# Graph attention, layer 2: weighted rows summed by VectorE and TensorE slot by slot, with a GpSimd memset at every sixth gather, in place of 32-node blocks summed on TensorE

## The chip, the cores and the metric

The kernel runs on one core of a Trainium2 chip. The core has five engines with an instruction stream each: TensorE (PE in the profile, its weight loads PEld), VectorE (DVE), ScalarE (ACT), GpSimd (POOL) and SyncE (SP). SP issues the plain DMAs; GpSimd issues the indirect ones, those that fetch or store rows by a list of row numbers. Both kinds are carried out by the same 16 DMA engines. The metric is the time of one execution on the device, in microseconds. Three runs of the kernel before took 5383.51, 5389.56 and 5395.65 us: a median of 5389.56.

## What is computed

Two graph attention layers over 10,000 nodes with 768 features and 170,000 edges (160,000 random ones and a self loop for each node), each with a layer norm and a residual, then a last layer norm:

```python
def gat_conv(x, edge_index, W, a_src, a_dst, bias, heads, out_ch, concat):
    ei = _add_self_loops(edge_index, n)
    src, dst = (ei[0], ei[1])
    xl = (x @ W).reshape(n, heads, out_ch)
    alpha_src = jnp.einsum('nhc,hc->nh', xl, a_src)
    alpha_dst = jnp.einsum('nhc,hc->nh', xl, a_dst)
    e = jax.nn.leaky_relu(alpha_src[src] + alpha_dst[dst], 0.2)
    m = jax.ops.segment_max(e, dst, num_segments=n)
    e = jnp.exp(e - m[dst])
    s = jax.ops.segment_sum(e, dst, num_segments=n)
    alpha = e / (s[dst] + 1e-16)
    msg = xl[src] * alpha[:, :, None]
    out = jax.ops.segment_sum(msg, dst, num_segments=n)
    ...
    return out + bias

h = gat_conv(x, edge_index, W1, a_src1, a_dst1, b1, 4, 256, True)      # layer 1
h = relu(layer_norm(h, g1, be1)) + (x @ Wr1 + br1)
h1 = h
h = gat_conv(h, edge_index, W2, a_src2, a_dst2, b2, 1, 768, False)     # layer 2
h = layer_norm(h, g2, be2) + (h1 @ Wr2 + br2)
x = _layernorm(x + h)
```

All of it is in float32. Layer 2 has one head of 768 columns: for each node, the rows of its sources are weighted with a softmax and summed.

## The kernel before, in words

**Preparation** (up to about 880 us). While TensorE computes x·W1 into table1, VectorE sorts the nodes by their number of edges. The sorted nodes are cut into 79 blocks of 128, one node to a partition. All nodes of a block get the same number of slots, SLOTS[t], from 8 to 41, 1377 in all; a slot that a node does not need points to an empty row. A slot is a row of 128 sources, one for each node of the block. The blocks are taken in the order TURNS: the sizes rise from 8 to 41 in blocks 0 to 39, and fall from 27 to 9 in blocks 40 to 78.

**Layer 1** (880 to about 3445 us) gathers a slot's 128 rows of table1 at a time into a ring of 29 slots, weighs them on ScalarE and VectorE, a part of them on TensorE, and then, in the same stretch, computes the block's rows of table2 (h1·W2, with two columns for the attention). It also stores h1 and x in the new order (h1_d, x_d). `logits` (L488 on) turns the numbers of a block's nodes into the lists of row numbers for layer 2 (L511).

**Layer 2** (`ordered_layer2`, to the end) has a ring of 41 slots of 770 + 1 columns. The first slot of each block holds the block's own rows, which lie together in table2, and comes by a plain DMA on SP's queue (L474). The other 1298 slots are gathers on GpSimd's queue (L445). `Ring.fetch(upto)` issues whatever is not issued yet; each gather waits until the slot it overwrites, 41 earlier, has been read. The order of all instructions is the order in which the program issues them (`manual_schedule`), engine by engine.

Within a block, the n slots are cut into u = n - 4w single ones and w waves of four. A single slot k is as above: partition p holds a source of node p. In a wave, the four slots are rearranged: slot g holds, for the 32 nodes of the quarter g of the block, four sources each. The list of numbers for this is `wide`, made of `slots` by 16 copies (L897). A block then goes like this:

- `exponents(t)` (L960 to L994): the attention logits, their maximum by node, the exponents. The maximum needs moves between quarters of the partitions, for which there are many small VectorE instructions.
- `weighed(t, e)`: VectorE writes `spots` (L1005), a 128x32 matrix for each wave slot that has the weight of each partition's row in its node's column, and adds up the single slots (L1014, L1012). The ring's column 770 is 1, so that the sum of weights comes along.
- `summed(t, spots, acc)`: TensorE multiplies spots with the ring's rows (L1026), four matmuls with 32 output rows for each half and wave, into PSUM.
- `residual(t + 1)` (L1036, L1038): TensorE computes x + h1·Wr2 for the next block, among the sums.
- `norms(t - 1)`, in three steps between these: sum of both parts (L1048), division and bias (L1052), layer norm (L588, L590, L601, L603, L604), the residual (L1056), the last layer norm, whose last step is on ScalarE (L1062), and the scatter into the output by GpSimd (L1063).

`ring.fetch` is called twice a block, after the single slots and after the sums. The first two blocks' x and h1 and a broadcast of br1 lie in the ring's last slots (from slot 35 on) until TensorE has read them.

For the lines after the change: `weigh` (L523), `logits` (L481 on), `normalised`, `norms` and `attend_parts` are shared helpers.

Of the kernel before, what the change touches and what calls it, by code (L numbers as in the profile page):

```python
# [49 lines left out]
QUAD = 32  # L50
# [28 lines left out]
def gnn_kernel(ctx, tc, x, x_cols, src, dst, src_col, dst_col, W1, a_src1, a_dst1, b1, g1, be1, Wr1, br1,  # L79
# [21 lines left out]
    WAVES = [(n - 1) // G for n in SLOTS]  # L101
    SINGLE = sum(n - G * w for n, w in zip(SLOTS, WAVES))
    COLUMN, ALONE, WAVE = [0] * TOTAL, [0] * NT, [0] * NT
    a = w = 0
    for t in TURNS:
        ALONE[t], WAVE[t], u = a, w, SLOTS[t] - G * WAVES[t]
        a, w = a + u, w + WAVES[t]
        COLUMN[FIRST[t]:FIRST[t] + SLOTS[t]] = (list(range(ALONE[t], a))
                                               + list(range(SINGLE + G * WAVE[t], SINGLE + G * w)))
# [87 lines left out]

    def runs(lo, hi):

        q = lo  # L200
        while q < hi:
            e = q + 1
            while e < hi and COLUMN[e] == COLUMN[e - 1] + 1:
                e += 1
            yield COLUMN[q], COLUMN[q] + e - q, q
            q = e

    def prepare():

        with tc.tile_pool(name="prep", bufs=1, side="right") as pool, \  # L210
# [172 lines left out]
            def listed(t, window):  # L383
# [16 lines left out]
                for i in range(m):  # L400
                    f = FIRST[t + i]
                    for c, d, q in runs(f + 1, f + SLOTS[t + i]):
                        nc.vector.tensor_scalar_add(slots[:, c:d], got[:, i, q - f - 1:q - f - 1 + d - c],
                                                    float(NP))
                    c = COLUMN[f]
                    nc.vector.tensor_copy(slots[:, c:c + 1], order[:, t + i:t + i + 1])
# [54 lines left out]
    class Ring:  # L461
# [4 lines left out]
        def __init__(self, pool, table, row, size, own, index, more=0):  # L466
            self.table, self.size, self.own, self.issued, self.index = table, size, own, 0, index
            self.row = row
            self.rows = pool.tile([P, size, row + more], F32, name="ring")

        def fetch(self, upto):
            for q in range(self.issued, min(upto, TOTAL)):
                if q in self.own:
                    nc.sync.dma_start(self.slot(q)[:, :self.row],  # L474
                                      self.table[self.own[q] * P:(self.own[q] + 1) * P, :])
                elif q < self.size or self.own:
                    gather(self.slot(q)[:, :self.row], self.table[:, :], self.index(q))
                else:
                    gather(self.slot(q)[:, :self.row], self.table[:, :], self.index(q), bounds_check=NP - 1,
                           oob_is_err=False)  # L480
                self.issued = q + 1  # L481
# [12 lines left out]
    def logits(small, ring, lo, hi, ad, heads, c, top=None):  # L494
# [14 lines left out]
        for a, b, rows in ring.parts(lo, hi):  # L509
            for i, j, q in runs(a, b):  # L510
                nc.vector.tensor_scalar(slots[:, i:j], rows[:, q - a:q - a + j - i, R1 - 1], -1.0, float(NP),  # L511
                                        op0=OP.mult, op1=OP.min)
            nc.vector.memset(rows[:, :, c + heads:], -BIG)
# [20 lines left out]
    def weigh(acc, row, e, dh, shared=False):  # L534


        if shared:
            c = e.shape[1] * dh
            nc.vector.tensor_add(acc[:, :c], acc[:, :c], row[:, :c])  # L539
            return  # L540
        for h in range(e.shape[1]):
            s = slice(h * dh, (h + 1) * dh)
            nc.vector.scalar_tensor_tensor(acc[:, s], row[:, s], e[:, h:h + 1], acc[:, s],  # L543
                                           op0=OP.mult, op1=OP.add)

    def attend_parts(small, ring, acc, h_, ad, bias, heads, dh, t, summed):
# [7 lines left out]
        for lo, hi in zip(cuts, cuts[1:]):  # L554
# [15 lines left out]
            sums, m = summed(lo, e)  # L570
            for q in range(lo + m, hi):
                shared = q >= lo + m + (hi - lo - m) // 3
# [3 lines left out]
            nc.vector.tensor_add(acc[:, :c], acc[:, :c], sums[:, :c])  # L576
            ring.fetch(hi + ring.size)
# [111 lines left out]
    SLOTS, FIRST, WAVES, ALONE, WAVE = ([v[t] for t in TURNS] for v in (SLOTS, FIRST, WAVES, ALONE, WAVE))  # L689
# [4 lines left out]
    def ordered_layer1():  # L694
        with tc.tile_pool(name="b1", bufs=1) as pool, tc.tile_pool(name="small1", bufs=2) as small, \
# [3 lines left out]
            ring = Ring(pool, table1, R1, RING1, {}, lambda q: slots[:, COLUMN[q]:COLUMN[q] + 1])  # L699
# [183 lines left out]
    def ordered_layer2():  # L883
        nonlocal ps_big
        with tc.tile_pool(name="b2", bufs=1) as pool, tc.tile_pool(name="small2", bufs=2) as small, \
                tc.tile_pool(name="ps_acc2", bufs=2, space=PSUM) as ps_acc, \
                tc.tile_pool(name="ps_q2", bufs=2, space=PSUM) as ps_big, tc.manual_schedule():
# [4 lines left out]
            QUADS = [slice(g * QUAD, (g + 1) * QUAD) for g in range(G)]  # L892
            wide = pool.tile([P, (TOTAL - SINGLE) // G, G], I32, name="wide")
            narrow = slots[:, SINGLE:].rearrange("p (j s) -> p j s", s=G)
            for s, to in enumerate(QUADS):
                for g, come in enumerate(QUADS):
                    nc.vector.tensor_copy(wide[to, :, g], narrow[come, :, s])  # L897
            own, at = {}, {}
            for t in range(NT):
                own[FIRST[t]] = TURNS[t]  # L900
                u = SLOTS[t] - G * WAVES[t]
                for k in range(SLOTS[t]):
                    j, g = WAVE[t] + (k - u) // G, (k - u) % G
                    c = ALONE[t] + k
                    at[FIRST[t] + k] = slots[:, c:c + 1] if k < u else wide[:, j, g:g + 1]
            ring = Ring(pool, table2, R2, RING2, own, at.get, more=1)
            assert max(SLOTS) <= RING2 and G * QUAD == P

            full = RING2 * (R2 + 1)
            rest, flat = full, ring.rows.rearrange("p k n -> p (k n)")  # L910
# [9 lines left out]
            whole = rest // (R2 + 1)  # L920
            assert SLOTS[0] <= whole and NT > 1
            nc.vector.memset(ring.rows[:, :whole, R2], 1.0)
# [9 lines left out]
            ring.fetch(whole)  # L932
            adds = [parts[4][:, :C2], parts[5][:, :C2]]
            for to, v in zip(adds, (shift, br2)):
                nc.sync.dma_start(to, bass.AP(tensor=v.tensor, offset=v.offset, ap=[[0, P], [1, C2]]))
# [3 lines left out]
            nc.vector.tensor_add(b2_b, b2_b, adds[0])  # L939
            nc.vector.tensor_add(be2_b, be2_b, adds[1])  # L940

            number = pool.tile([P, 1], F32, name="number")
            nc.gpsimd.iota(number, pattern=[[0, 1]], base=0, channel_multiplier=1,
                           allow_small_or_imprecise_dtypes=True)
            quad = pool.tile([P, G], F32, name="quad")
            mask = pool.tile([P, QUAD], F32, name="mask")
            for g, s in enumerate(QUADS):
                nc.vector.tensor_scalar(mask[s], node[s, s], number[s], None, op0=OP.is_equal)
            nc.vector.memset(quad, 0.0)
            for g, s in enumerate(QUADS):  # L950
                nc.vector.memset(quad[s, g:g + 1], 1.0)
# [425 lines left out]
```

## Time and profile before

| what | value |
|---|---|
| three runs, us | 5383.51, 5389.56, 5395.65 |
| the profiled execution: time, span | 5383.51, 5381.6 |
| granted clock of TensorE | 0.934 |
| busy in the span, us | PE 4604.0, PEld 2427.2, DVE 3856.7, ACT 2741.2, POOL 3296.9 |
| layer 2's gathers on GpSimd, mean ns | 118 of single slots 998 to 1017, 1180 of waves 1014 |
| first gather of layer 2 starts, last one starts | 3445.03, 5313.94 |
| last scatter starts | 5369.81 |

The span is that of one execution of the program, the one that was profiled, and its time is that of the same execution. A line of a timeline gives the start, the length, the engine, the source line, the operation, what it writes and reads, and in brackets how long the engine was idle before and what released it. A line of groups gives the count, the busy time and mean ns, and the idle time before. A line of waits says which line waited for which, us in total, how many times, and the longest. "issue" is idle time in which the engine waited for nothing that the profile shows. GpSimd counts as busy only while it makes a gather's descriptors, not in the gap after it.

### The profile page before, as it was taken

Reading aid. Unit: us, or ns where it says so; the run is one execution under the profiler, and the core shown is the slowest. Engines: PE = TensorE matmul, PEld = TensorE weight load, DVE = VectorE, ACT = ScalarE, POOL = GpSimd, SP = SyncE. Lnnn points to the kernel's source line nnn. Section 1 sums busy time; section 2 is a strip of 40 time slices with the busy share of each in tenths; the row PEclk is TensorE's granted clock in tenths of the full one; section 3 lists DMA queues with packets and bytes.
Section 4 is the critical chain, followed back from the end, with each engine's and each line's share of the span. In section 5 each row is a group of like instructions: output and inputs, shape, how many; then the busy total and the mean of one; then the engine's idle time right before and its main releaser. Section 6 shows DMA issues by size and latency. Waiting matters only on the chain. (4 is left out here: it accounts for less than half of the span.)

```text
span 5381.6 us, 61043 instructions
## 1 busy us (share of the span) xinstructions
PE 4604.0 (86%) x16999; PEld 2427.2 (45%) x16999; DVE 3856.7 (72%) x8213; ACT 2741.2 (51%) x6878; POOL 3296.9 (61%) x3160
## 2 busy tenths in 40 slices
PE   8999996999999887578999999788877766778887
PEld 3444443555555544345555555444433322333343
DVE  5884254899999887788899999577655433465677
ACT  3434443787888876778888888322211111111122
POOL 3446455555666664656666555267777767777774
PEclk9999998999999988789999999899998878889899
DMA  4333625899999996789999999589999989999995
GB/s 155 125 98 88 92 93 213 300 339 345 358 357 368 356 343 248 288 331 346 358 370 354 354 336 321 198 305 359 355 352 352 347 281 343 343 349 356 367 358 224
DMA packets 474309, 1591.47 MB, mean 296 GB/s; under 512 B 118327, under 2 KB 122487, under 8 KB 473958
## 3 DMA queue, kind: packets, MB, share of 16 engines
q0 software_dynamic: 322384, 1286.62, 65.7%
q1 hardware_dynamic: 149520, 297.43, 16.1%
q10 hardware_dynamic: 2054, 3.42, 0.2%
q8 instruction: 137, 2.24, 0.2%
q14 instruction: 214, 1.75, 0.1%
HBM read 1431.80 MB, written 177.29 MB: 299 GB/s over the span
## 5 line engine op out<-in xcount | busy, mean ns | idle before, releaser
L445 POOL DMA_INDIRECT ring<-table,slots x1495 | 1520.0, 1017 | 1012.0 <-issue 230.3
L445 POOL DMA_INDIRECT ring<-table,wide x1180 | 1196.2, 1014 | 387.6 <-issue 189.1
L532 ACT ACTIVATE ring<-ring,e 128x256 f32<-128x256 f32 x3284 | 1337.9, 510 | 0.0
L539 DVE TENSOR_TENSOR acc<-acc,ring 128x1024 f32<-128x1024 f32 x801 | 985.7, 1231 | 79.1 <-ACT ring L532 10.1
L1038 PE MATMUL big<-wr,w 128*128 128x512 f32 (+1 forms) x2464 | 888.0, 509 | 0.0
L179 PE MATMUL big<-w,xT 128*128 128x512 f32 x1896 | 825.7, 597 | 23.3 <-DMA w<-in_W_dram 9.7
L179 PE MATMUL big<-wr,xT 128*128 128x512 f32 x1896 | 833.6, 596 | 0.2 <-ACT xT L715 0.2
L832 PE MATMUL half<-w,hT 128*128 128x512 f32 (+1 forms) x2528 | 830.4, 486 | 0.0
L543 DVE SCALAR_TENSOR_TENSOR acc<-ring,e,acc 128x256 f32<-128x256 f32 x1232 | 602.3, 489 | 82.4 <-PE acc L744 43.0
L1026 PE MATMUL acc<-ring,spots 128*32 128x512 f32 (+1 forms) x4720 | 471.6, 534 | 215.6 <-issue 176.6
L744 PE MATMUL acc<-ring,diagonals 128*128 128x256 f32 x1912 | 483.3, 411 | 200.8 <-ACT diagonals L738 200.5
L1038 PEld LDWEIGHTS big<-wr,w 128*128 128x128 f32 x2464 | 482.1, 198 | 371.6 <-issue 340.6
L832 PEld LDWEIGHTS half<-w,hT 128*128 128x128 f32 x2528 | 477.8, 189 | 372.8 <-issue 310.4
L179 PEld LDWEIGHTS big<-w,xT 128*128 128x128 f32 x1896 | 361.7, 192 | 483.0 <-issue 462.2
L592 ACT ACTIVATE sd<-mv,eps 128x1 f32<-128x1 f32 x237 | 69.8, 295 | 977.5 <-DVE mv L590 977.5
L179 PEld LDWEIGHTS big<-wr,xT 128*128 128x128 f32 x1896 | 356.9, 192 | 420.4 <-issue 419.8
L744 PEld LDWEIGHTS acc<-ring,diagonals 128*128 128x128 f32 x1912 | 390.8, 207 | 285.6 <-ACT diagonals L738 223.4
L1026 PEld LDWEIGHTS acc<-ring,spots 128*32 128x32 f32 x4720 | 148.6, 116 | 553.6 <-issue 464.0
L676 DVE TENSOR_TENSOR scr<-big,ad_b 128x1024 f32<-128x1024 f32 x79 | 96.7, 1224 | 372.9 <-ACT row L673 372.9
L738 ACT ACTIVATE diagonals<-ident,e 128x128 f32<-128x128 f32 x956 | 292.8, 387 | 116.8 <-DVE e L523 116.4
L960 DVE COPY e<-ring 128x15 f32<-128x15 f32 (+22 forms) x110 | 21.9, 200 | 457.4 <-DMA ring<-table,wide 262.3
L681 POOL TENSOR_TENSOR row<-row,none 128x1024 f32<-128x1024 f32 x79 | 187.4, 2372 | 262.3 <-ACT row L673 261.9
(201 smaller groups left out, 4497.2 us busy)
## 6 DMA issues: line engine op xcount, KB each, us to landing
table<-row SPq DMA_DIRECT2D x79, 516.0 KB, 3.6
h_d<-hT SPq DMA_DIRECT2D x79, 512.0 KB, 7.2
w<-h_d SPq DMA_DIRECT2D x77, 512.0 KB, 7.9
table<-row SPq DMA_DIRECT2D x79, 385.0 KB, 6.3
ring<-table SPq DMA_DIRECT2D x79, 385.0 KB, 6.2
xT<-in_x_cols_dram SPq DMA_DIRECT2D x79, 384.0 KB, 4.4
x_d<-xt SPq DMA_DIRECT2D x79, 384.0 KB, 6.6
w<-x_d SPq DMA_DIRECT2D x77, 384.0 KB, 10.3
```

The lines of the kernel that those rows point to most:

```text
L179: nc.tensor.matmul(p[:, c:e], aT[:, j, :], w[:, j, c:e], start=(j == 0), stop=(j == k - 1))
L445: nc.gpsimd.indirect_dma_start(out=to, out_offset=None, in_=table, in_offset=bass.IndirectOffsetOnAxis(ap=index, axis=0), **more)
L532: nc.scalar.activation(row[:, s], row[:, s], AF.Copy, scale=e[:, h:h + 1])
L539: nc.vector.tensor_add(acc[:, :c], acc[:, :c], row[:, :c])
L543: nc.vector.scalar_tensor_tensor(acc[:, s], row[:, s], e[:, h:h + 1], acc[:, s], op0=OP.mult, op1=OP.add)
L676: nc.vector.tensor_mul(m, p[:, :C1], vec)
L681: nc.gpsimd.tensor_add(row[:, :C1], row[:, :C1], b1_b)
L738: nc.scalar.activation(diagonals[:, k * H1 + i, :], ident, AF.Copy, scale=e[:, k, i:i + 1])
L744: nc.tensor.matmul(acc[:, c:d], diagonals[:, k * H1 + i, :], ring.slot(q + k)[:, c:d], start=(k == 0 and c % BANK == 0), stop=(k == m - 1 ...
L832: nc.tensor.matmul(q, hT[:, j, :], w2[:, j, c:c + q.shape[1]], start=(j == 0), stop=(j == K1 - 1))
L1026: nc.tensor.matmul(acc[s, c:d], spots[:, G * j + g, :], ring.slot(q + G * j + g)[:, c:d], start=(j == 0), stop=(j == w - 1), skip_group_ch ...
L1038: nc.tensor.matmul(r[:, c:d], hT[:, j, :], wr2[:, j, c:d], start=False, stop=(j == K1 - 1), skip_group_check=True)
```

## The change

The waves and everything for them go (`wide`, COLUMN, `exponents`, `weighed`, `summed`, the 771st column). Slots are all of the single kind. The 768 columns are split: VectorE sums columns 0 to 511 slot by slot, with the accumulator in PSUM (`weigh`, L523, 128x512), and TensorE sums columns 512 to 767, with a diagonal matrix of weights for each slot that ScalarE makes (a copy of the identity, scaled, 128x128), into free columns of the residual's PSUM tile (a matmul of 128x256). The weights are divided by their sum beforehand (`normalised`). The weights of block t + 1 are made within block t's loop, at slot `turn` and LEAD = 3 slots later; the three steps of `norms(t - 1)` stand ahead of the loop and at slots 3, 6 and 9 (the scatter). `ring.fetch` is called after each slot, so that a slot's successor can be issued as soon as VectorE has weighed it. And `fetch`, in layer 2 alone (`self.own`), issues on GpSimd a memset of a 128x512 buffer, which nothing reads, ahead of every slot whose number divides by six.

In layer 1 the lists of row numbers stand in the order of the slots again, so that L511 is one instruction for a stretch instead of two or more.

```diff
-QUAD = 32
+DIAGONALS = 5
+ON_PE2 = 512
...
-        def __init__(self, pool, table, row, size, own, index, more=0):
-            self.table, self.size, self.own, self.issued, self.index = table, size, own, 0, index
-            self.row = row
-            self.rows = pool.tile([P, size, row + more], F32, name="ring")
+        def __init__(self, pool, table, row, size, own):
+            self.table, self.size, self.own, self.issued = table, size, own, 0
+            self.rows = pool.tile([P, size, row], F32, name="ring")
+            if own:
+                self.idle = pool.tile([P, BANK], F32, name="idle")

         def fetch(self, upto):
             for q in range(self.issued, min(upto, TOTAL)):
+                if self.own and q % 6 == 0:
+                    nc.gpsimd.memset(self.idle, 0.0)
                 if q in self.own:
...
-                    gather(self.slot(q)[:, :self.row], self.table[:, :], self.index(q))
+                    gather(self.slot(q), self.table[:, :], slots[:, q:q + 1])
...
         for a, b, rows in ring.parts(lo, hi):
-            for i, j, q in runs(a, b):
-                nc.vector.tensor_scalar(slots[:, i:j], rows[:, q - a:q - a + j - i, R1 - 1], -1.0, float(NP),
-                                        op0=OP.mult, op1=OP.min)
-            nc.vector.memset(rows[:, :, c + heads:], -BIG)
+            if not ring.own:
+                nc.vector.tensor_scalar(slots[:, a:b], rows[:, :, R1 - 1], -1.0, float(NP), op0=OP.mult, op1=OP.min)
+                nc.vector.memset(rows[:, :, c + heads:], -BIG)
...
-            nc.vector.scalar_tensor_tensor(acc[:, s], row[:, s], e[:, h:h + 1], acc[:, s],
-                                           op0=OP.mult, op1=OP.add)
+            nc.vector.scalar_tensor_tensor(acc[:, s], row[:, s], e[:, h:h + 1],
+                                           (acc if first is None else first)[:, s], op0=OP.mult, op1=OP.add)
...
-                tc.tile_pool(name="ps_q2", bufs=2, space=PSUM) as ps_big, tc.manual_schedule():
+                tc.tile_pool(name="ps_q2", bufs=3, space=PSUM) as ps_big, tc.manual_schedule():
...
+            def weights_of(t):
+                n = SLOTS[t]
+                ad = small.tile([P, H2], F32, name="ad")
+                nc.vector.tensor_add(ad, ring.slot(FIRST[t])[:, C2:C2 + H2], lift)
+                e, _ = logits(small, ring, FIRST[t], FIRST[t] + n, ad, H2, C2)
+                yield e
+                normalised(small, e, H2, t)
+                to = rs[t][:, C2:2 * C2 - ON_PE2]
+                nc.tensor.matmul(to, ones, b2_b[0:1, ON_PE2:], start=False, stop=False, skip_group_check=True)
+                for k in range(n):
+                    if k % G == 0:
+                        diagonals = pool.tile([P, G, P], F32, name="diagonals", bufs=DIAGONALS)
+                    nc.scalar.activation(diagonals[:, k % G, :], ident, AF.Copy, scale=e[:, k, :])
+                    nc.tensor.matmul(to, diagonals[:, k % G, :], ring.slot(FIRST[t] + k)[:, ON_PE2:C2],
+                                     start=False, stop=(k == n - 1), skip_group_check=True)
+                yield
...
+            def norms(t, h, r, means):
+                stats = deviation(small, [a for m in means for a in pieces(m, C2 - ON_PE2)])
+                yield
+                scaled(h, means, stats, g2_b, be2_b)
+                nc.vector.tensor_add(h, h, r[:, :C2])
+                mean, inv = deviation(small, pieces(h, C2 // 2))
+                yield
+                nc.vector.reciprocal(inv, inv)
+                less = small.tile([P, 1], F32, name="less")
+                nc.vector.scalar_tensor_tensor(less, mean, -1.0, inv, op0=OP.mult, op1=OP.mult)
+                o = pool.tile([P, C2], F32, name="out")
+                nc.scalar.activation(o, h, AF.Identity, bias=less, scale=inv)
+                yield
                 nc.gpsimd.indirect_dma_start(
...
             for t in range(NT):
+                n = SLOTS[t]
+                if 0 < t < NT - 1:
+                    rs[t + 1] = residual(t + 1)
...
+                    e = (ready or list(weights_of(t)))[0]
+                    acc = ps_acc.tile([P, BANK], F32, name="acc")
+                    if not t:
+                        rs[1] = residual(1)
+                        ring.fetch(RING2)
+                    next(last, None)
+                    ready, ahead, turn = [], iter(()), n
+                    if t + 1 < NT and SLOTS[t + 1] + LEAD <= ring.size:
+                        ahead = weights_of(t + 1)
+                        turn = min(max(n // 3, n + SLOTS[t + 1] + 2 * LEAD - ring.size), n - LEAD)
+                    for k in range(n):
+                        if k in (turn, turn + LEAD):
+                            ready += itertools.islice(ahead, 1)
+                        if k in (LEAD, 2 * LEAD, 3 * LEAD):
+                            next(last, None)
+                        weigh(acc, ring.slot(FIRST[t] + k), e[:, k], ON_PE2, None if k else b2_b)
+                        ring.fetch(FIRST[t] + k + 1 + ring.size)
+                        if t + 2 < NT and k == n // 2:
+                            ins[t + 2] = fetch_x(t + 2)
+                    ready += ahead
+                    for _ in last:
+                        pass
```

## The prediction

> **What bounds the kernel now.** I began with the windows view, cut at the layers' borders: preparation and x·W1 to 880 us, layer 1 to 3445, layer 2 to the end. Only layer 2 changes in earnest.
>
> ```profile
> 880.00:3445.00 2565.00, 2256.75 (x7442) 1350.59 (x7442) 2237.33 (x3758) 2041.01 (x5033) 1478.66 (x1456) 0.95 0.90 331
> 3445.00:5315.00 1870.00, 1462.89 (x7399) 683.23 (x7400) 1084.55 (x3279) 329.94 (x451) 1390.38 (x1373) 0.89 0.94 345
> ```
>
> Columns: stretch, length, then busy us (instructions) of PE, weight loads, DVE, ACT and GpSimd, then clock, DMA share, GB/s. In layer 2 GpSimd's 1390 us look like 74%. They aren't, as its timeline shows:
>
> ```profile
> 3489.51 0.94 POOL L445 DMA_INDIRECT ring<-table,wide  x1 [0.30 <-DMA ring<-table,wide]
> 3490.76 0.95 POOL L445 DMA_INDIRECT ring<-table,wide  x1 [0.30 <-issue]
> 3491.71 0.16 POOL L943 IOTA number<- 128x1 f32 x1
> 3492.03 0.96 POOL L445 DMA_INDIRECT ring<-table,wide  x1 [0.16 <-issue]
> ...
> 4006.37 0.95 POOL L445 DMA_INDIRECT ring<-table,wide  x1 [0.30 <-PE acc L1026]
> 4007.62 1.49 POOL L445 DMA_INDIRECT ring<-table,wide  x1 [0.30 <-issue]
> 4009.41 0.95 POOL L445 DMA_INDIRECT ring<-table,wide  x1 [0.30 <-DMA ring<-table,wide]
> ```
>
> A gather takes 0.95 us, and 0.30 us always pass before the next, whoever is named: 1.253 us is GpSimd's floor per gather. Hence GpSimd is nearly full, and issuing bounds layer 2. The 1.49 us gather answers to DVE's timeline at that moment:
>
> ```profile
> 4007.29 1.01 DVE L601 SCALAR_TENSOR_TENSOR w<-w,mv,g 128x768 f32<-128x768 f32 x1
> ```
>
> It started at 4007.62, and instead of 0.95 it took 0.54 more, about what L601 had still to run (0.68, to 4008.30). L601 reads two SBUF tensors. DVE steps with one of them in PSUM (L1048, L1056) go with no long gathers. Blocked time in layer 2 is, from the windows view of L445 alone:
>
> ```profile
> 3445.00:5315.00 1870.00, 1313.84 (x1298) 0.89 0.94 345
> ```
>
> 1313.84 - 1298 x 0.949 (the median) = 82 us. So GpSimd, from its first gather's start (3445.0) to its last one's (5313.9), 1869 us: 1298 x 1.253 = 1626; 74 scatters L1063 between them x 1.33 (1.03 + 0.30) = 98; blocked 82; the remaining 63 are waits. Of these the page of waits names the large ones (0.30 of each is the usual gap):
>
> ```profile
> POOL out_dram L1063 <- ACT w L1062: 77.0, 12, 24.1
> ...
> POOL ring L445 <- PE big L1036: 16.5, 16, 12.0
> ...
> POOL ring L445 <- DVE ring L1098: 8.6, 1, 8.6
> ```
>
> 20 us at the head, where the ring's last slots still hold x and h (L1036, L1098); 24 us once, before the block of 41 slots (the rest of that line lies after the last gather); 19 scattered. From the last gather's start to the last scatter's are 55.9 us, then 11.8 to the end.
>
> **The change, part by part.** All against this execution (span 5381.6, time 5383.5; the median shown is 5389.6, 6 us above it, so I add differences to the median).
>
> *Memsets.* q % 6 == 0 over 1377 slots: 230 memsets of 128x512 on GpSimd's queue, ahead of whatever is queued there (gathers, scatters); their own wait is on the memset before, long done. The rows are
>
> ```profile
> masks.py:197 POOL MEMSET ident<- 128x128 f32 x1 | 0.2, 205 | 0.3 <-POOLq L1369 0.3
> ...
> L1369 POOL MEMSET const-float32-0.0<- 128x1 f32 x1 | 0.1, 99 | 0.2 <-issue 0.2
> ```
>
> (205 - 99)/127 = 0.83 ns a column, so 512 columns take 0.525 us. The IOTA above shows how a short step sits between gathers: it starts as the gather ends and leaves a 0.16 gap, so it costs its length + 0.16 - 0.30. Net 0.385 us x 230 = 89 us. Ends: 0.065 each (as short as 128 columns) = 15 us, and 1.05 each (half of L681's 2.37 us for 1024 columns, net) = 241 us. I take 89, a memset's own row.
>
> *Gathers.* Still 1298 of 128 rows and the same bytes; index columns come from slots instead of wide. 0 us. The spacing gives DMA room it does not lack while GpSimd is late.
>
> *Blocked time.* L1012, L1052, L601 (with h in SBUF) and L1005 go. Per block only L604's form (1.02) and the first weighing, which adds b2 (0.75), read two SBUF tensors; the others have the accumulator or the residual in PSUM. Layer 1 already works so, DVE being busy 2237 of 2565 us there: its gathers, median 0.992 and mean 1.017, lose 0.025 each. x 1298 = 32 us, for 82: -50. Ends: 0, and 82 unchanged; if it went with DVE's busy time, 82 x 1750/1085 = 132. I take 32, from the nearest form.
> The Trainium skill, "SBUF — State Buffer", section "Who interferes with whom", says that a DVE instruction with two SBUF inputs contends with GpSimd instructions that read SBUF, not with those that only write it. That fits the 1.49 row. By the rule a memset is never held, and blocked time falls; by the bare row, scaled with DVE's busy time, it would grow to 132 and the sum below end 100 us higher. It also makes the pair a lock, which speaks against a memset: a DVE copy would wait for one; layer 2 afterwards has no copies in its loop.
>
> *Waits.* Head: residual(1) is issued right after block 0's weights and no longer after block 0's L1085, so x leaves the ring at about 3494 as GpSimd arrives: 20 becomes 5. Block of 41: it still has to land whole (the last one issued 4405.1, read at 4414.4, 9.3 us), then exponents and the first weighing, 4 us: 24 becomes 14. New: the next block's logits are read when only six gathers beyond its rows may be issued (turn, 2·LEAD). 6 x 1.34 = 8.0 us cover a landing (5 to 7 us in the middle blocks) and 2.1 us of DVE, or miss it by up to 1: 10 us over the 22 blocks of 20 slots or more. Scattered 19 stay. 63 becomes 48, between 35 and 80.
>
> *Sum on GpSimd:* 1626 + 98 + 32 + 89 + 48 = 1893, for 1869: +24.
>
> *DVE* takes over all 1377 rows. L543 (128x256, PSUM accumulator) is 0.489 and L601 on a PSUM accumulator of 1024 is 1.284, so 512 columns are 0.755, + 0.035 gap = 0.79: 1088 us. Per block besides: three BN_STATS of 256 columns 1.2, aggregation, L601 in two pieces, reciprocal, L604, adding r, two BN_STATS, aggregation and small ones 5.0, logits and normalising 2.2, in all 8.4 x 79 = 664. Together 1752 us, against 1085 now. It starts at about 3473 (when b2 has landed, as now) and has 1893: 93% full, covered by GpSimd, but not by much. In blocks under 15 slots (0.79n + 8.4 against GpSimd's 1.32n + 0.5) DVE is the slower by 1 to 3 us; the ring's 41 slots absorb that at the start; at the end it adds to the tail. Tail: DVE 10 us behind, landing 5.5, half of block 77, block 78 and three norms 33, ACT 1.6, together 50, and up to 59 if the store of one block holds the next; now 55.9. 0.
>
> *PE and ACT.* 4720 spots matmuls (472 us) go, 1377 of 128x256 (0.41, 0.21 when packed as L744) come; 1377 diagonals at 0.387 = 533 us on ACT, which with the rest is under 900 of 1870. Hidden under GpSimd; if that cover went, ACT's 11 us a block are still half of a block's 24. SP issues the same loads in another order: br2's waits for the sum of b2 and shift (3472), and the own rows of blocks 1 to 3 stand behind it. They land near 3480, before DVE is through block 0 (3483): 0, at worst 5 us while GpSimd still fills the ring. The scatter now stands in GpSimd's queue behind nine more gathers, by when ACT has long written its tile: 0.
>
> *Layer 1 and the wide table.* About 100 index conversions L511 fewer at 0.07 us where they follow each other, at most 7 us, on a DVE 87% full beside DMA at 0.90: -3. The 16 copies L897 delayed the first wide gather by 2 us: -2. (0 to -9 together.)
>
> Total: +24 - 5 = +19 on the median of 5389.6: **5409 us**.
>
> **Rivals.** *Faster:* GpSimd absorbs the memset in the 0.30 us gap, at the price of the 128-column row (15 instead of 89): -74, 5335. It decides below 0.30 us net a memset. For it: half the IOTA vanished in that gap. Against: the rest of it did not. *Blocked time stays at 82:* +50, 5459. Against it: layer 1's rows. *DVE becomes the bound:* L539 after L539 left 0.10 us gaps instead of 0.035. At 0.90 us a row DVE needs 1903 from 3473, and with 30 at the block of 41 and 13 at the end it comes to 5419 of the span: +37, 5427. It decides from 0.88. Against it: L539 also waits for ACT; L543 after L543, with one wait as here, left 0.035. *Memset dearer:* net 1.05, +152 more, 5561. *It makes no difference:* 5389, if the waits stay shorter than I put them (48 becomes 30); the terms nearly cancel (+89 against -50 and -15), so this is the lower part of the forecast's own range.
>
> **How the numbers follow.** Issue stays the bound with about these terms (5380 to 5435): 0.42; faster rival 0.24; blocked stays 0.11; DVE binds 0.15; memset dearer 0.08. A measurement of this kernel can tell about 0.2%, 11 us (here three runs lie 12 us apart). Of the 0.42 some 0.15 lie below 5400: same 0.16 with a little of DVE's case; faster 0.26, slower 0.58. Leaving out 0.1 on either side: 5325 to 5480.
>
> **What would show it.** Right: gathers 0.95 with 0.30 gaps, memsets near 0.53, layer 2's GpSimd window about 1890 long with few gathers over 1.1; DVE some 1750 busy, waiting at L481 for ring rows. Wrong: GpSimd's gathers waiting for DVE's L523 in mid-layer (DVE binds), memsets far from 0.53, or long gathers during L523.

## The result, and the profile after

The changed kernel took 5416.6 us (median of four executions, 5410.2 to 5421.7), the kernel before in the runs beside it 5390.9: a ratio of 1.0048, 95% interval 1.0031 to 1.0066. That is 26 us more, for 19 forecast. The profiled execution took 5410.21 us, with a span of 5408.4.

The windows view of the kernel after, cut where its layer 2 ends; columns as before (PE, weight loads, DVE, ACT, GpSimd, then clock, DMA share, GB/s):

```profile
880.00:3445.00 2565.00, 2259.53 (x7449) 1350.41 (x7450) 2233.80 (x3679) 2040.23 (x5029) 1485.59 (x1461) 0.95 0.90 331
3445.00:5340.00 1895.00, 1632.71 (x5626) 1113.06 (x5625) 1545.56 (x3197) 730.60 (x1798) 1451.65 (x1596) 0.92 0.94 339
```

Layer 1 is as it was. In layer 2 VectorE goes from 1085 to 1546 us busy and TensorE from 1463 to 1633, but the stretch is only 25 us longer, which speaks against either of them setting its length. GpSimd's timeline in mid-layer shows a queue that is nearly full:

```profile
4004.78 0.95 POOL L424 DMA_INDIRECT ring<-table,slots  x1 [0.31 <-DVE acc L523]
4006.04 0.95 POOL L424 DMA_INDIRECT ring<-table,slots  x1 [0.30 <-PE big L931]
4006.99 0.54 POOL L454 MEMSET idle<- 128x512 f32 x1
4007.69 0.95 POOL L424 DMA_INDIRECT ring<-table,slots  x1 [0.16 <-PE big L931]
```

The gathers follow each other with the bare 0.30 us gap, and a memset stands between two of them as the IOTA did before: it starts as the gather ends, takes 0.54, and leaves a gap of 0.16. The groups of GpSimd's lines in layer 2 (count, busy us, mean ns, idle before):

```profile
L424 POOL DMA_INDIRECT ring<-table,slots x1298 | 1255.8, 968 | 422.3 <-issue 117.5 <-DVE acc L523 87.9 <-PE big L931 86.4
L454 POOL MEMSET idle<- 128x512 f32 x230 | 125.8, 547 | 58.7 <-DMA table<-row 58.6
```

1298 gathers took 1255.8 us, for 1313.8 before: with the same median of 0.949, blocked time is 24 us instead of 82. So, between the starts of the first and the last gather of layer 2, from the two profiled executions:

| us | before | after, forecast | after, measured |
|---|---|---|---|
| length | 1869 | 1893 | 1900.5 |
| 1298 gathers x 1.253 and 74 scatters | 1724 | 1724 | 1724 |
| blocked | 82 | 32 | 24 |
| memsets, net | 0 | 89 | 93 (230 x 0.405) |
| waits over the usual gaps | 62 | 48 | 59 |
| last gather to last scatter | 55.9 | 55.9 | 54.9 |

The net price is 0.545 (median) + 0.165 - 0.305 = 0.405 us. The waits are the row that is furthest off. Two lines of GpSimd's waits in layer 2 (us in total, times, longest; 0.30 of each is the usual gap):

```profile
POOL ring L424 <- DVE acc L523: 87.9, 193, 13.2
POOL ring L424 <- PE big L931: 86.4, 249, 14.7
```

The longest of each, 13.2 and 14.7, are both at the block of 41 slots, where there was one wait of 24.1 before: 27 us over the usual gaps, for 14 forecast. Fifteen waits of 1.1 to 2.8 us, one a block in the blocks of about 20 slots or more, add 23, for 10 forecast. The other 9 are small.

### The profile page after: what moved, and what is told of

The parts are those of the page before. It is cut to its first block, busy times and chain, and to the rows that moved or that the text cites. A ratio compares the mean times of both kernels' runs of the same rounds, so it can differ in the third digit from the quotient of the medians.

```text
span 5408.4 us, 60267 instructions
## 1 busy us (share of the span) xinstructions
PE 4778.5 (88%) x15191; PEld 2864.1 (53%) x15191; DVE 4313.8 (80%) x7966; ACT 3150.0 (58%) x8255; POOL 3367.0 (62%) x3389
## 5 line engine op out<-in xcount | busy, mean ns | idle before, releaser
L424 POOL DMA_INDIRECT ring<-table,slots x2675 | 2660.9, 995 | 1332.5 <-DVE acc L523 313.9
L523 DVE SCALAR_TENSOR_TENSOR acc<-ring,e,acc 128x512 f32<-128x512 f32 (+1 forms) x2530 | 1577.9, 624 | 118.8 <-PE acc L732 43.3
L931 PE MATMUL big<-ring,diagonals 128*128 128x256 f32 x2754 | 698.4, 417 | 250.6 <-ACT diagonals L930 236.4
L945 PE MATMUL big<-wr,w 128*128 128x512 f32 (+1 forms) x2464 | 822.0, 487 | 0.0
L931 PEld LDWEIGHTS big<-ring,diagonals 128*128 128x128 f32 x2754 | 573.0, 211 | 373.9 <-ACT diagonals L930 274.6
L945 PEld LDWEIGHTS big<-wr,w 128*128 128x128 f32 x2464 | 469.3, 190 | 329.1 <-issue 297.2
L930 ACT ACTIVATE diagonals<-ident,e 128x128 f32<-128x128 f32 x1377 | 410.9, 387 | 127.5 <-DVE e L503 118.6
L580 ACT ACTIVATE sd<-mv,eps 128x1 f32<-128x1 f32 x237 | 69.8, 295 | 606.8 <-DVE mv L578 606.5
L726 ACT ACTIVATE diagonals<-ident,e 128x128 f32<-128x128 f32 x956 | 292.8, 388 | 116.5 <-DVE e L503 116.2
L667 ACT ACTIVATE scr<-scr 128x256 f32<-128x256 f32 x632 | 253.6, 403 | 120.3 <-DVE scr L664 120.3
```

The costliest lines, as they stand in the source:

```text
L424: nc.gpsimd.indirect_dma_start(out=to, out_offset=None, in_=table, in_offset=bass.IndirectOffsetOnAxis(ap=index, axis=0), **more)
L667: nc.scalar.activation(m[:, s], m[:, s], AF.Copy, accum_out=row[:, C1 + i * H1 + h:C1 + i * H1 + h + 1])
L726: nc.scalar.activation(diagonals[:, k * H1 + i, :], ident, AF.Copy, scale=e[:, k, i:i + 1])
L930: nc.scalar.activation(diagonals[:, k % G, :], ident, AF.Copy, scale=e[:, k, :])
L931: nc.tensor.matmul(to, diagonals[:, k % G, :], ring.slot(FIRST[t] + k)[:, ON_PE2:C2], start=False, stop=(k == n - 1), skip_group_check=True)
L945: nc.tensor.matmul(r[:, c:d], hT[:, j, :], wr2[:, j, c:d], start=False, stop=(j == K1 - 1 and (d < C2 or not whole(t))), skip_group_check= ...
```

## Experiments

Twelve runs, in three sets of four, each set on a chip of its own. In the second and third set the kernel before took 5390 us, as in the result above. In the first it took 5717.9 (eight executions, 5707.7 to 5723.3); layer 1 ended there as elsewhere (layer 2's first gather at 3452 to 3457 us in the profiles of that set), so that the difference lies in layer 2. That set is told last. Each ratio is to the kernel before of its own set.

| kernel | us | ratio, 95% interval |
|---|---|---|
| after, again | 5422.2 | 1.0061 (1.0044 to 1.0078) |
| after, no memsets | 5355.8 | 0.9939 (0.9922 to 0.9955) |
| after, memset at every third slot | 5492.4 | 1.0190 (1.0173 to 1.0207) |
| before, with memsets | 5470.7 | 1.0151 (1.0134 to 1.0168) |
| after, accumulator in SBUF | 5555.3 | 1.0312 (1.0295 to 1.0329) |
| after, late norms | 5407.6 | 1.0032 (1.0021 to 1.0044) |
| no memsets, late norms | 5344.3 | 0.9912 (0.9896 to 0.9929) |
| the same, logits later | 5304.5 | 0.9838 (0.9822 to 0.9855) |

### What a memset costs

The kernel after as it stands, as the control:

> The kernel after, unchanged, as the control of the runs beside it. In the first four experiments the kernel before took 5718 us instead of 5390, all the difference in layer 2, where more than before of the transfers of table2's rows took over 0.4 us. Where the kernel before takes about 5390: 1.005 of it. Where it takes about 5718: between the kernels without memsets (5652) and with twice as many (5572), about 5610, 0.981 of it.

It took 5422.2 us, 1.006 of the kernel before. Without the memsets:

```diff
-                if self.own and q % 6 == 0:
-                    nc.gpsimd.memset(self.idle, 0.0)
```

> The kernel after without the memsets, once more. Theory (two regimes: GpSimd's issue binds where the transfers keep up, and there a memset costs 0.405 us; late landings bind where they don't, and there it costs nothing or helps): where the kernel before takes about 5390, 5324 to 5345, 0.988 to 0.992 of it and 70 to 93 us under the kernel after; where it takes about 5718, 0.990 again and above the kernel after. Rival (the spacing by memsets helps the transfers everywhere): above the kernel after in either case.

With twice as many:

```diff
-                if self.own and q % 6 == 0:
+                if self.own and q % 3 == 0:
```

> The kernel after with the memset at every third slot (459 instead of 230). Theory (GpSimd's issue binds; a memset costs 0.405 us less what waits give back): from none to 230 it cost 66 us, 93 of price less 27 of waits that shrank; the waits still left in the large blocks (about 25 us) can give back at most that, so 70 to 93 more than the kernel after, 5490 to 5510 where the kernel before takes about 5390, 1.019 to 1.023 of it. Rival (the price flattens, because a slower GpSimd lets the landings keep up): under 40 more. Where the kernel before takes about 5718: 0.975 again.

5355.8, 5422.2 and 5492.4 us for 0, 230 and 459 memsets: 66 us for the first 230 and 70 for the next 229. (The last kernel is of the third set, where the kernel before took 5390.1, for 5390.0 in the second.) The 70 lie in the range expected. The 66 miss theirs, 70 to 93, from below: too little was put down to the waits. Both are the 93 us of the price less what comes back as shorter waits, apart from small changes in the length of the gathers. Without memsets (first), and with the 230 of the control (after it), the groups of GpSimd's lines are:

```profile
L424 POOL DMA_INDIRECT ring<-table,slots x1298 | 1246.5, 960 | 552.1 <-DVE acc L521 118.8 <-PE big L929 103.9 <-issue 103.7
```

```profile
L424 POOL DMA_INDIRECT ring<-table,slots x1298 | 1260.0, 971 | 423.9 <-issue 126.3 <-DVE acc L523 84.5 <-PE big L931 83.8
L454 POOL MEMSET idle<- 128x512 f32 x230 | 125.8, 547 | 58.9 <-DMA table<-row 58.8
```

From the first gather's start to the last one's: 1837.5 us without and 1904.3 with them, 67 apart. (The two spans lie only 61 apart, as what follows the last gather is 8 us longer without memsets, and the first gather comes 2 us earlier.) Of the 93, 37 came back as waits (98 us over the usual gaps without memsets, 61 with them), and blocked time was 14 lower without (15 against 28). Most of those 37 are the waits once a block in the blocks of 20 slots and more, counted where they are over 1 us: 50 us together with no memsets, 22 with 230, 9 with 459. They shrink as GpSimd slows down, and at 459 there is little left of them to give back. The rival, that the pause is worth its time to the transfers, falls in this set.

The memset alone, in the kernel before:

```diff
             for q in range(self.issued, min(upto, TOTAL)):
+                if self.own and q % 6 == 0:
+                    nc.gpsimd.memset(self.idle, 0.0)
```

> The kernel before with the memset ahead of every sixth slot. Theory (issue binds before as well): +93 less at most 20, 5463 to 5483 where the kernel before takes about 5390, 1.0135 to 1.0175 of it; the rest of the change is then worth 40 to 60 by itself. Rival (the kernel before waits for landings or VectorE in layer 2 and a memset fits in): within 20 of the kernel before. Where the kernel before takes about 5718: 0.9945 again.

5470.7 us, 81 more than the kernel before. So the change consists of 230 memsets that cost 66 to 81 us together, by the base that they are put on, and of the rest, which is worth 34 us without them (5355.8 against 5390.0) and, across sets, 48 to 54 with them (5422.2 and 5416.6 against 5470.7).

### Where the blocked time went

The accumulator of VectorE's sums goes from PSUM into SBUF, and the memset's buffer is 64 columns shorter to make room for it:

```diff
-                self.idle = pool.tile([P, BANK], F32, name="idle")
+                self.idle = pool.tile([P, BANK - 64], F32, name="idle")
...
-                    acc = ps_acc.tile([P, BANK], F32, name="acc")
+                    acc = pool.tile([P, BANK], F32, name="acc", bufs=2)
```

> The kernel after, with layer 2's accumulator in SBUF instead of PSUM, so that each of the 1377 weighings reads two SBUF tensors (the memset has 448 columns instead of 512 to make room, 12 us less at most). Theory (a gather that starts while VectorE works on two SBUF tensors is held until that ends): VectorE is in such steps for 0.55 to 0.6 of the time, a held gather loses half a step, 0.35 us: blocked time from 24 us to between 110 and 240, 80 to 200 us more than the kernel after, and VectorE's busy time within 5%. Rival (long gathers have another cause, and the fall of 58 us came from the smaller number of VectorE's small steps or from the index columns): blocked time stays near 24 and the time near the kernel after.

133 us more than the control. The gathers' and memsets' groups, and four lines of the timeline:

```profile
L424 POOL DMA_INDIRECT ring<-table,slots x1298 | 1411.9, 1088 | 406.0 <-issue 118.5 <-PE big L931 85.4 <-DVE acc L523 69.7
L454 POOL MEMSET idle<- 128x448 f32 x230 | 113.5, 493 | 58.8 <-DMA table<-row 58.7
```

```profile
4032.79 1.02 DVE L592 SCALAR_TENSOR_TENSOR w<-w,sd,be 128x768 f32<-128x768 f32 x1
...
4033.41 1.22 POOL L424 DMA_INDIRECT ring<-table,slots  x1 [0.30 <-issue]
...
4034.83 1.02 DVE L576 BATCH_NORM_STATS2 st<-w 128x6 f32<-128x384 f32 x2
...
4035.28 0.95 POOL L424 DMA_INDIRECT ring<-table,slots  x1 [0.17 <-issue]
```

The gathers' busy time rose by 152 us, from 1260.0 to 1411.9, which makes 180 us blocked; 548 of them took over 1.1 us instead of 56. The scatters between them took 13 us longer in all; the shorter memsets give back 12 and the waits 18, which makes, within 1 us, the 134 by which the stretch from the first to the last gather grew. The gather at 4033.41 started 0.40 us before the end of L592, which reads two SBUF tensors, and took 0.27 more than usual; the one at 4035.28 ran beside BN_STATS, which reads one, and took 0.95. So it is the kind of VectorE's step that lengthens a gather, not VectorE's being busy: VectorE's weighings took a mean of 0.744 us here and 0.748 in the control, and between the first and the last gather it was busy for 1548 us in both. For steps of this form it is the inputs that count, and not where the result goes. Of the control's gathers, those that had a certain step of VectorE beside them 0.13 us after their start took this much longer than 0.949 us, on average: 0.002 us beside a weighing with the accumulator in PSUM (650 gathers), 0.003 beside L955, which reads one tensor of SBUF and writes SBUF (28), but 0.23 beside a block's first weighing, which reads two and writes PSUM (39), and 0.31 beside L592 (52). Two SBUF tensors are not the only thing that holds a gather, though: in the kernel before, 33 gathers beside L1014, which multiplies one row of the ring with a column of weights, took 0.20 us longer, 7 of its 82 us. The memsets were not held: 0.493 for 448 columns, where the control's 0.547 for 512 would give 0.479 by length. That agrees with the Trainium skill, "SBUF — State Buffer", section "Who interferes with whom", by which a step with two SBUF inputs disturbs a GpSimd instruction that reads SBUF and not one that only writes it. The same section calls the shared port a lock that blocks whichever comes second; here only the gathers grew, the weighings not.

### The block of 41

GpSimd (first), VectorE (second) and ScalarE (third) at that block, in the kernel after's timelines:

```profile
4411.59 0.95 POOL L424 DMA_INDIRECT ring<-table,slots  x1 [13.24 <-DVE acc L523]
4412.85 0.94 POOL L424 DMA_INDIRECT ring<-table,slots  x1 [0.30 <-DVE w L589]
4428.52 0.95 POOL L424 DMA_INDIRECT ring<-table,slots  x1 [14.73 <-PE big L931]
```

```profile
4405.93 0.17 DVE L481 TENSOR_TENSOR e<-ring,ad 128x6 f32<-128x6 f32 x1 [9.41 <-DMA ring<-table,slots]
...
4423.65 0.16 DVE L591 RECIPROCAL sd<-sd 128x1 f32<-128x1 f32 x1 [10.97 <-ACT sd L580]
```

```profile
4421.61 0.40 ACT L930 ACTIVATE diagonals<-ident,e 128x128 f32<-128x128 f32 x1 [0.45 <-PE big L931]
4422.03 1.28 ACT L580 ACT_TABLE_LOAD   x1
4423.33 0.29 ACT L580 ACTIVATE sd<-mv,eps 128x1 f32<-128x1 f32 x1
```

The first stall is the block's landing, as forecast. The second is new: the standard deviation of the block before (L580) stands on ScalarE behind all 41 diagonals of this block, VectorE waits 11 us for it ahead of its fourth weighing, and no slot comes free. Because the ring has 41 slots and the block needs all of them, its weights can't be made ahead; in every other block the diagonals are issued in the block before. The experiment keeps all work and moves the norm around the diagonals:

```diff
-                    e = (ready or list(weights_of(t)))[0]
+                    late = not ready and t > 0
+                    steps = iter(()) if ready else weights_of(t)
+                    ready = ready or [next(steps)]
+                    e = ready[0]
+                    if late:
+                        next(last, None)
+                    for _ in steps:
+                        pass
...
-                    next(last, None)
+                    if not late:
+                        next(last, None)
...
-                        if k in (LEAD, 2 * LEAD, 3 * LEAD):
+                        if k in ((n - 15, n - 12, n - 9) if late else (LEAD, 2 * LEAD, 3 * LEAD)):
```

> The kernel after, with one block's order changed: at the block of 41 slots, whose weights can't be made ahead, the preceding block's first step of norms is issued before the 41 diagonals, and its other steps come 15, 12 and 9 slots before the end instead of at slots 3, 6 and 9. Theory (in the profile after, VectorE waits 10.97 us there for sd L580, which stands on ScalarE behind the 41 diagonals, and GpSimd's second stall, 14.7 us, is that wait): the second stall goes, 11 to 14 us less than the kernel after beside it, in either regime. Rival (the stall is TensorE's work on the 41 diagonals, which holds the slots whatever VectorE does): 0 to -3.

```profile
4410.64 0.95 POOL L424 DMA_INDIRECT ring<-table,slots  x1 [0.17 <-issue]
4426.02 0.94 POOL L424 DMA_INDIRECT ring<-table,slots  x1 [14.43 <-PE big L931]
4427.26 0.95 POOL L424 DMA_INDIRECT ring<-table,slots  x1 [0.30 <-DVE acc L523]
4428.51 0.95 POOL L424 DMA_INDIRECT ring<-table,slots  x1 [0.30 <-PE big L931]
```

14.6 us less than the control, a little over the 11 to 14 expected, and the second stall is gone. ScalarE's 41 diagonals took as long as before (14.4 us from the first to the last, 13.7 in the kernel after), and the slots came free while they were in work: it was the norm behind them. The first stall stays, 14.4 for 13.2.

Both gains together:

> The kernel after without the memsets and with the order of f3 at the block of 41. Theory (both gains lie on GpSimd's path, at different places): 66 + 14.6 less than the kernel after, about 5341, 0.991 of the kernel before where that takes 5390. Rival (without the memsets the landings bind, and the second stall at the block of 41 is given back in the blocks after it): 5350 to 5356.

5344.3 us: 11 less than without the memsets alone, across two sets in which the kernel before took the same time, and 18 less by the two profiled executions (5361.2 and 5343.0), for 14.6 expected. The gains add, as far as these runs can tell.

### The waits in the large blocks

In the kernel without memsets, VectorE and GpSimd at a block of 22 slots:

```profile
4189.96 0.15 DVE L919 TENSOR_TENSOR ad<-ring,lift 128x1 f32<-128x1 f32 x1
4196.81 0.19 DVE L479 TENSOR_TENSOR e<-ring,ad 128x22 f32<-128x22 f32 x1 [6.70 <-DMA ring<-table,slots]
```

```profile
4194.15 0.95 POOL L424 DMA_INDIRECT ring<-table,slots  x1 [0.30 <-PE big L943]
4199.06 0.95 POOL L424 DMA_INDIRECT ring<-table,slots  x1 [3.96 <-DVE acc L521]
```

VectorE has stopped weighing to read the next block's logits and waits until that block's last slot has landed; GpSimd runs out of free slots meanwhile. In the kernel after it is the same: at fourteen of its fifteen waits of this kind VectorE stood idle at L481 for 4.5 to 8.6 us, put down to a landing. The six slots that it may fill in that time are 2·LEAD:

```diff
-                        turn = min(max(n // 3, n + SLOTS[t + 1] + 2 * LEAD - ring.size), n - LEAD)
+                        turn = min(max(n // 3, n + SLOTS[t + 1] + 3 * LEAD - ring.size), n - LEAD)
```

> As g3, and the next block's logits are read when nine gathers beyond its rows may be issued instead of six (3*LEAD in place of 2*LEAD in turn), which concerns the blocks of about 20 slots or more. Theory (the 1 to 4 us that GpSimd waits once a block there, in all some 60 us without memsets, is VectorE waiting at its logits for the landing of the block's last slot, while GpSimd may issue only six more): three more gathers are 3.75 us, more than nearly all of these waits: 30 to 50 less than g3, 5290 to 5311. Rival (the landing itself is late because the transfers are at their limit, DMA share 0.95): within 10 of g3, and the waits move to other slots.

Two lines of the waits over blocks of that kind (4060 to 4800 us), first for the kernel with 2·LEAD, then with 3·LEAD, both without memsets and with the late norms:

```profile
DVE e L479 <- DMA ring<-table,slots: 125.7, 21, 12.4
POOL ring L424 <- DVE acc L521: 72.5, 95, 4.4
```

```profile
DVE e L479 <- DMA ring<-table,slots: 90.2, 21, 13.0
...
POOL ring L424 <- DVE acc L521: 26.5, 79, 1.7
```

5304.5 us, 40 less than beside it, and GpSimd's waits for VectorE's weighings in that stretch fall from 72.5 to 26.5 us. The transfers were not at a limit: in that stretch they went from 326 to 345 GB/s. This version beats the kernel before by 1.6% (1.5 to 1.8) and the kernel after by about 2%.

### The same on a chip where layer 2 was slower

The first, second and fourth run have edits that are shown above: no memsets, a memset at every third slot, and the kernel before with memsets. The third fills only 128 of the memset's 512 columns.

> The kernel after, without the memsets. Theory (GpSimd's issue binds, and a memset costs it 0.545 + 0.165 - 0.305 = 0.405 us net): 230 x 0.405 = 93 us less, 5417 - 93 = 5324, or up to 5345 where the small blocks' VectorE work (1634 us busy in a window of then 1808) can't follow. Rival (the pause is what lets transfers or VectorE keep up): the time freed comes back as waits of gathers for VectorE's L523 or for landings, 5390 or more.

> The kernel after, with the memset at every third slot (459 instead of 230). Theory (each memset is paid on GpSimd's queue): +229 x 0.405 = +93, 5510, less up to 25 of waits that a slower GpSimd no longer has (the 1 to 3 us waits in the large blocks, and part of the wait at the block of 41): 5485 to 5510. Rival (the memset is hidden beside a bound on VectorE or DMA): under 5440.

```diff
-                    nc.gpsimd.memset(self.idle, 0.0)
+                    nc.gpsimd.memset(self.idle[:, :P], 0.0)
```

> The kernel after, with the memset on 128 of its 512 columns. Theory (the price goes by the memset's length): 0.205 + 0.165 - 0.305 = 0.065 net, 15 us for 230, so 78 less: 5339, a little above the kernel without memsets. Rival (the price is per instruction, not by length, as where the descriptor work restarts after each memset): about 5417.

> The kernel before, with a memset of 128x512 on GpSimd ahead of every sixth slot of layer 2. Theory (issue binds there too): +93, less what the 61.8 us of waits over the usual gaps absorb (20 at most): 5465 to 5483. Rival (before, GpSimd waits for others, and a memset fits in): under 5430. If both this and the kernel after without memsets go as the theory says, the rest of the change is worth about -65 to -90 by itself.

Here the kernel before took 5717.9 us, and memsets were a gain: without them 5652.5 us (0.9896, 0.9879 to 0.9912), with 230 of 128 columns 5637.7 (0.9869, 0.9846 to 0.9891), with 459 of 512 columns 5571.7 (0.9752, 0.9733 to 0.9771), and the kernel before with memsets 5678.4 (0.9945, 0.9926 to 0.9965). None of the four went as the theory had it: for the kernel without memsets, for example, it had 5324 to 5345 us. The kernel after itself was not run there. The 128-column memset took 0.224 us there, with the same gaps; as a test of the price by length it is spoilt, since the price was not what bound.

What differs is on TensorE. The matmuls of one residual (L943), which have nothing to wait for once the first has run, in the kernel without memsets, here (first) and in the second set (after it):

```profile
4732.65 1.01 PE L943 MATMUL big<-wr,w 128*128 128x512 f32 x1 [1.80 <-issue]
4735.44 1.01 PE L943 MATMUL big<-wr,w 128*128 128x512 f32 x1 [1.78 <-issue]
4737.55 1.01 PE L943 MATMUL big<-wr,w 128*128 128x512 f32 x1 [1.10 <-issue]
```

```profile
4533.53 7.03 PE L943 MATMUL big<-wr,w 128*128 128x512 f32 x16
```

Sixteen such matmuls go through in 7.03 us in the second set, and here there are gaps of 1 to 2 us between single ones. Counting gaps of over 0.25 us within rows of this line, between layer 2's first and last gather: 130 gaps, 144 us, without memsets; 113 gaps, 72 us, with 459 memsets; none in the second set. GpSimd's waits over the usual gaps are 390 us without memsets and 112 with 459, for 98 without memsets in the second set; the largest part of the 390, 166 us, is put down to the diagonals' matmuls, which free the ring's slots (22 of the 98 in the second set). So there GpSimd waits mostly for a late TensorE, and with memsets on its queue these waits and TensorE's gaps are both shorter. That TensorE sets layer 2's length there is read from the waits; no run changed TensorE's part.

Why its matmuls come late is open. "Issue" means only that the profile shows no cause. It is not the landings, as the expectations of the second set had it: by the packets' times a gather's rows had landed 3.6 us (median) after the gather's end here, 4.4 in the second set. Nor is it the larger share of the gathers' packets that took over 0.4 us, 9.3% here against 5.7%: the kernel with the accumulator in SBUF had 9.6% in the second set and none of these gaps. Nor is it the clock: TensorE was granted half its clock for 521 us between these gathers, for 280 in the second set, but the kernel with the accumulator in SBUF had 451 us of it without a gap, and of the 144 us of gaps 93 lie where the full clock was granted.

## Why the prediction came out right

*What binds.* Right: GpSimd's queue sets layer 2, shown by the price of memsets that are added or taken away, on either base.

*Memsets.* Right: 0.525 forecast for 0.545, net 0.385 for 0.405, 89 us for 93, from a row of 128 columns and one of a single column. The faster rival, a memset that vanishes in the gap between gathers, needed less than 0.30 net and falls; the dearer memset falls as well. But 93 us on the queue are 66 in the time of this kernel, since 37 come back as waits, and some 14 are lost again to longer gathers. The forecast's sum, which puts all of it into the length and forecasts the waits apart, allows for that only within the waits' term.

*Blocked time.* Right: 32 forecast, 24 measured, and the mechanism is shown by putting one operand back into SBUF. Of the 24, 13 lie beside L592 and 8 beside the first weighings, the two forms that the forecast named. Its list of the steps that go leaves out L1014, one of those that had held gathers before. That blocked time goes by the kind of VectorE's steps and not by its busy time decided 100 us of the forecast.

*Waits.* The mis-sized term: 48 forecast, 59 measured. Two of its steps failed. "Block of 41 ... 24 becomes 14": it became 27, because "*PE and ACT* ... Hidden under GpSimd" compared ScalarE's busy time with the layer's length, and did not ask what stands behind the 41 diagonals in its queue. "10 us over the 22 blocks": it was 23. The price of the landing and VectorE's work beyond it was put at a miss of up to 1 us a block, and it was 0.8 to 2.5 in fifteen of them. In return the head and the scattered waits came to 9 instead of 24, which is luck as far as the sum goes.

*VectorE.* Right that it is covered. From the first gather to the end of the kernel it was busy for 1598 us, where the forecast had 1752 for all 79 blocks: 48 of the difference are the 0.035 gaps, which busy time does not count, 10 are the weighings, and the rest is 7.2 us of other work a block instead of 8.4. The forecast's "93% full" set the work of all blocks against GpSimd's stretch, though a part of it comes behind the last gather; between the first and the last gather VectorE was busy for 1547 of 1900 us. The rival that it binds falls: even without memsets it was busy for 1541 of 1838 us. The sign that the prediction gave for this rival, gathers that wait for L523 in mid-layer, did appear, but there VectorE was itself waiting for landings, and the run with later logits took most of these waits away.

*Tail, head.* 54.9 us from the last gather to the last scatter, for 55.9: 0 as forecast. Layer 2's first gather came 4.1 us earlier, -5 forecast; but in the control it came at 3450.5, so that 4 us are within what it scatters by.

*The sum.* +31.6 in the window, -4.1 before it and -0.8 behind it make +26.7, the difference of the two profiled executions (5410.2 - 5383.5); medians differ by 25.7, for +19. The excess over the forecast is the 11 us of waits, less 4 of the blocked time and the memsets together. The terms were off by +11, -8 and +4 us, so that the sum is nearer than its parts by some luck.

## What to carry over

Where a queue that issues transfers is the bound, price an added instruction by its length plus the gap that it leaves less the gap that it fills, and then look for the waits that shrink as the queue slows: they give a part back, until they are used up. An in-order engine that is half idle can still stop another: ask what small result stands behind its long row of work, above all at the one block that breaks the usual order. And take VectorE's second operand from PSUM where GpSimd issues gathers beside it.

## What was not expected of the hardware

The same programs had two regimes on different chips: layer 2 of the kernel without memsets took 1838 us from first to last gather in one and 2127 in the other, with layer 1 unchanged (first gather at 3448.5 and 3452.3). In the second, TensorE's matmuls that depend on nothing came with gaps of up to 3.1 us, and 459 idle memsets on GpSimd made the kernel 1.4% faster. Memsets that cost 66 to 81 us on the other chips were a gain there, and no run here says why, nor whether it goes with the chip or with the time of the runs.
